# Holding first statistics behind an earlier supertile's places, and starting expert blocks one round earlier, in a fused AdaLN, scan and mixture-of-experts kernel

## Chip, cores and metric

The kernel runs on one core of a Trainium2 chip. The metric is the device time in microseconds. Before the change three executions took 446.07, 444.80 and 445.12 us; the median is 445.12 us. A time is called different here when it differs by more than 0.3%, 1.3 us.

## What is computed

32 sequences of 256 tokens with 128 channels, float32. Two layers, each behind a normalization that is modulated by a small conditioning vector:

```
mod = silu(c) @ wmod                        # six vectors for each sequence
h   = layernorm(x) * (1 + ca) + sa
g, a, v = sigmoid(h Wg' + bg), sigmoid(h Wd' + bd), h Wv' + bv
x   = x + ga * (scan(h_t = a_t h_{t-1} + (1 - a_t) v_t) * g)
h   = layernorm(x) * (1 + cb) + sb
logits = h @ gate_w' + gate_b               # 8 experts, the best 2 of a token
x   = x + gb * sum over 2 experts of prob_e * (relu(h w1[e] + b1[e]) w2[e] + b2[e])
```

Each token goes to its two best experts only, so the kernel has to sort tokens by expert, multiply, and bring the results back.

## The kernel before, in words

The 8192 tokens are cut into 16 **supertiles** of 512. A supertile passes four steps, which the code calls n, m, r and R:

- **n**, `a_norm` (L343): the statistics of the first normalization on VectorE (`stats` L303: four `bn_stats`, L307, and four `bn_aggr`, L311), a reciprocal root in some eleven small VectorE operations (`rsqrt`, L315 to L336), and four ScalarE activations that make `xn` (L355). Supertiles 12 and 13, and 14 and 15, share one root (`LN1G`, L62).
- **m**, `a_mix` (L364): transposes, three matmuls `pz` (L377), gates, and the scan on VectorE (L396).
- **r**, `a_res` (L400): the residual, the second statistics `stb`/`mvb` and root, and `xm` on ScalarE (L413).
- **R**, `a_route` (L416): logits on TensorE (`pl`, L428), best two experts, prefix counts (`pq`, L454), and then the **place** of each pair of token and expert in a region in DRAM. The cast to `pi` (L471) ends the placing. Eight indirect DMAs on GpSimd then scatter 128 rows each to `reg` (`send` L482, issued at L499).

`HEAD` (L33) writes down the first rounds: `n0|m0 n1|r0 m1 n2|R0 r1 m2 n3|...`. Round t handles n of supertile t, m of t-1, r of t-2 and R of t-3. In the first seven rounds R comes first in its round; from round 7 on n comes first and R last. r, m and R carry a priority ahead of program order (`AHEAD`, L39), n does not. The instructions of each engine are put into a fixed order when the program is built, by priorities and an estimate of times; on the chip each engine runs its list in order.

Routed rows are used in **blocks** of 256 rows of one expert. `b_load` (L579) has SyncE fetch the block's rows (`xr`, L584) and its expert's weights (`ww`, L590); `b_in` (L593) transposes and splits the rows (`xs`), `b_up` (L608) is twelve matmuls and the relu, `b_down` (L628) sixteen matmuls and the scaling `yt` (L639), and two scatters of results to `yd` on GpSimd. A load waits for the last sixteen row scatters that were sent before it in the program (L586). A row fetch is not told apart by expert: any of these rows could belong to it.

`b_step` (L729) runs one step of the block pipeline: loads up to four blocks ahead, `b_in` of block i, `b_up` of i-1, `b_down` of i-2. Between the supertile steps `between()` calls it, from round `FIRST` on, except at every eighth place, and only while more than two blocks are known and not begun. Blocks become known when supertiles 2 to 8, 10 and 12 are routed and their rows sent (`TAKE`, L30). `drip` (L507) sends row scatters, a few after each supertile step.

All scatters, of rows and of results, are chained in one written order (`scatter`, L497), and GpSimd runs them one after another. After the last route the remaining blocks run one after another; then SyncE loads the two results of each token (`c_load` L698) and VectorE adds them to x (`c_add` L709).

The lines that the change touches, in `stats`, `a_norm` and `a_route`:

```python
w = nc.vector.bn_stats(st[:, j], src[:, j])                       # L307
if behind:
    tc.add_manual_dep(w.ins, behind.name, ORDER, ...)             # L309
...
stats(mv[:, i * T:(i + 1) * T], xa[:, s + i], f"a{s + i}", placed[-1] if placed else None)   # L348
...
w = nc.vector.tensor_copy(pi, pf.rearrange("p t k -> p (t k)"))   # L471
if s < EARLY:
    placed.append(w.ins)
```

`ORDER` is an order on the same engine, without a semaphore: the statistics stand behind that cast in VectorE's list. `EARLY` is 3, so `placed` holds the casts of supertiles 0, 1 and 2.

Of the kernel before, what the change touches and what calls it, by code (L numbers as in the profile page):

```python
# [17 lines left out]
ORDER = mybir.DependencyInfo(mybir.DependencyClass.NoSync, mybir.DependencyReason.DATA)  # L18
# [8 lines left out]
T = 4  # L27
# [6 lines left out]

XE = 3
EARLY = 3
PW = 3

AHEAD = (0, 200, 300, 400)  # L39
# [1 line left out]
BACK = 2  # L41
SKIP = 8

FIRST = 6
THREE = 7

ALWAYS = 68
# [18 lines left out]
def adaln_moe(ctx: ExitStack, tc: tile.TileContext, x, Wg, bg, Wv, bv, Wd, bd,  # L66
# [16 lines left out]
    of = out.rearrange("b s d -> (b s) d")  # L83
# [23 lines left out]
    xa = cp.tile([P, NS, T, D], F32, name="xa")  # L107
# [189 lines left out]
    f = nc.sync.dma_start(reg[E * CAP:E * CAP + BLK].rearrange("(p t) d -> p t d", p=P), pad)  # L297
# [5 lines left out]
    def stats(mv, src, name, behind=None):  # L303
        n = src.shape[1]
        st = wk.tile([P, T, 6], F32, tag=f"st{name[0]}", name=f"st{name}")
        for j in range(n):
            w = nc.vector.bn_stats(st[:, j], src[:, j])  # L307
            if behind:
                tc.add_manual_dep(w.ins, behind.name, ORDER, reason="not ahead of the first supertiles that route")  # L309
        for j in range(n):  # L310
            nc.vector.bn_aggr(mv[:, j], st[:, j])  # L311

    def rsqrt(mv, name, s):

        n = mv.shape[1]  # L315

        def t1(nm, dt=F32):
            return wk.tile([P, n, 1], dt, tag=f"{nm}{name[0]}{n}", name=f"{nm}{name}")

        v, y, r = t1("nv"), t1("ny"), t1("nr")  # L320
        if s < PW:
            nc.vector.tensor_scalar(v, mv[:, :, 1:2], 1e-5, RSQ ** -2, op0=ALU.add, op1=ALU.mult)
            nc.gpsimd.tensor_tensor(y, v, mh[:, :n], op=ALU.pow)
        else:
            t = t1("nt")
            nc.vector.tensor_scalar(v, mv[:, :, 1:2], 1e-5, None, op0=ALU.add)
            nc.vector.tensor_scalar(y.bitcast(I32), v.bitcast(I32), 1, None, op0=ALU.logical_shift_right)
            nc.vector.tensor_scalar(y.bitcast(I32), y.bitcast(I32), -1.0, float(0x5f3759df), op0=ALU.mult, op1=ALU.add)
            nc.vector.tensor_tensor(t, y, y, op=ALU.mult)
            nc.vector.tensor_tensor(t, t, v, op=ALU.mult)  # L330
            nc.vector.scalar_tensor_tensor(t, t, -10.0 / 3.0, t, op0=ALU.add, op1=ALU.mult)
            nc.vector.scalar_tensor_tensor(y, t, 5.0, y, op0=ALU.add, op1=ALU.mult)
            nc.vector.tensor_tensor(t, y, y, op=ALU.mult)
            nc.vector.scalar_tensor_tensor(t, t, -0.5 * RSQ ** -2, v, op0=ALU.mult, op1=ALU.mult)
            nc.vector.scalar_tensor_tensor(y, t, 1.5, y, op0=ALU.add, op1=ALU.mult)
        nc.vector.scalar_tensor_tensor(r, mv[:, :, 0:1], -1.0, y, op0=ALU.mult, op1=ALU.mult)  # L336
        return y, r


    placed = []  # L340
    ln1 = {}

    def a_norm(s):  # L343
        g = LN1G.get(s, 0)
        if g:
            mv = wk.tile([P, g * T, 2], F32, tag=f"mva{g}", name=f"mva{s}")
            for i in range(g):
                stats(mv[:, i * T:(i + 1) * T], xa[:, s + i], f"a{s + i}", placed[-1] if placed else None)  # L348
            y, r = rsqrt(mv, f"a{s}", s)
            for i in range(g):  # L350
                ln1[s + i] = (y[:, i * T:(i + 1) * T], r[:, i * T:(i + 1) * T])
        y, r = ln1[s]
        xn = wk.tile([P, T, D], F32, tag="xn", name=f"xn{s}")
        for j in range(T):
            nc.scalar.activation(xn[:, j], xa[:, s, j], AF.Identity, scale=y[:, j], bias=r[:, j])  # L355
        return dict(s=s, xn=xn)

    def early(s, tag, name, bufs=1):

        if s < EARLY:  # L360
            return psb.tile([P, ST], F32, tag=tag, name=name, bufs=bufs)
# [38 lines left out]
    def a_res(a):  # L400
        s, og = a["s"], a["og"]
        xt = xa[:, s]
        po = early(s, "pbx", f"po{s}")
        for j in range(T):
            nc.tensor.transpose(po[:, j * P:(j + 1) * P], every(og, j), ident)
        xm = xt.rearrange("p t d -> p (t d)")
        nc.vector.tensor_tensor(xm, po, xm, op=ALU.add)
        mv = wk.tile([P, T, 2], F32, tag="mvb", name=f"mvb{s}")
        stats(mv, xt, f"b{s}")
        y, r = rsqrt(mv, f"b{s}", s)  # L410
        xn = wk.tile([P, T, D], F32, tag="xm", name=f"xm{s}")
        for j in range(T):
            nc.scalar.activation(xn[:, j], xt[:, j], AF.Identity, scale=y[:, j], bias=r[:, j])  # L413
        a["xn"] = xn

    def a_route(a, base):  # L416
        s, xn = a["s"], a["xn"]
# [51 lines left out]
        nc.vector.tensor_reduce(pf, op_, axis=AX.X, op=ALU.add)  # L469
        pi = wk.tile([P, T * K], I32, tag="pi", name=f"pi{s}", bufs=3)  # L470
        w = nc.vector.tensor_copy(pi, pf.rearrange("p t k -> p (t k)"))  # L471
        if s < EARLY:
            placed.append(w.ins)
        sm = wk.tile([P, T], F32, tag="sm", name=f"sm{s}")
        nc.vector.tensor_reduce(sm, e8, axis=AX.X, op=ALU.add)
        rc = wk.tile([P, T], F32, tag="rc", name=f"rc{s}")
# [30 lines left out]
    def drip(n):  # L507
        for _ in range(min(n, len(sending))):
            s, send, j, k = sending.pop(0)
            w = send(j, k)  # L510
            sent.append(w)
            if not sending or sending[0][0] != s:
                while held and held[0][0] <= s:
                    blocks.extend(held.pop(0)[1])
# [252 lines left out]
    def between():  # L767
        nonlocal slot
        slot += 1
        if slot % SKIP and len(blocks) - len(flow) > BACK:  # L770
            b_step()
# [19 lines left out]
    for t, todo in enumerate(steps):  # L791
        def step3(s):
            nonlocal base, done
            with tc.high_priority(AHEAD[3] * (s >= EARLY)):
                base = a_route(st[s], base)
                if s in CLS:
                    b = cp.tile([P, E], F32, name=f"cnt{s}")
                    nc.vector.tensor_copy(b, base)  # L798
                    base = b
                    counts.append(b)  # L800
                nb = len(blocks) + sum(len(x) for _, x in held)
                if s in TAKE:
                    n = full(s) - nb
                    tb, done = table(s, counts[:1] * (s > CUT) + [base], done, n, False)
                    held.append((s, [(tb, q, []) for q in range(n)]))
                elif s == NS - 1:
                    n = touched(s) - nb
                    tb, done = table(NS, counts, done, n, True)
                    fills(base)
                    rest = [(tb, q, []) for q in range(n)]  # L810
                    held.append((s, rest))
                    z = 0
                    for c in CLS:
                        u = max(E, touched(c) - nb) if c == CUT else touched(c) - nb
                        rest[u - 1][2].extend(range(z, c + 1))
                        z = c + 1

        def step2(s):
            with tc.high_priority(AHEAD[2] * (s >= EARLY)):
                a_res(st[s])  # L820

        def step1(s):
            with tc.high_priority(AHEAD[1] * (s >= EARLY)):
                a_mix(st[s])

        def step0(s):
            with tc.high_priority(AHEAD[0] * (s >= EARLY)):
                st[s] = a_norm(s)

        for i, s in todo:  # L830
            (step0, step1, step2, step3)[i](s)
            drip(3 if t < THREE else 2 if len(sending) > K * T else 1)
            if t >= FIRST:
                between()
# [59 lines left out]
```

## Time and profile before

| | us |
|---|---|
| median of the runs | 445.12 |
| the profiled execution | 444.96 |
| its span, first to last instruction | 443.2 |
| TensorE busy / weight loads | 366.6 / 321.5 |
| VectorE busy | 326.2 |
| ScalarE busy | 291.5 |
| GpSimd busy | 285.0 |
| one scatter of rows, mean, x128 | 0.986 |
| one scatter of results, mean, x136 | 1.013 |
| mean granted TensorE clock | 0.904 of full speed |

How to read it: the span is one execution as the profiler of the chip saw it; what the measured time has more, 1.76 us, lies before the first and behind the last instruction. A busy share is an average over stages. In this kernel they differ: a head in which supertiles are normalized and routed and no block is ready (to about 95 us), a long middle in which routes and blocks share the engines (to about 320), blocks alone (to about 375), and blocks beside the sums. PE in the profile is TensorE's matmuls, PEld its weight loads, DVE is VectorE, ACT ScalarE, POOL GpSimd, SP SyncE. The page's slices cut the span in 40 pieces of 11.08 us and give the busy tenths of each.

Places (the cast of L471) and first row scatters of the first supertiles, from the timeline:

| supertile | place, start us | first row scatter, start us |
|---|---|---|
| 2 | 65.33 | 66.27 |
| 3 | 88.08 | 89.00 |
| 4 | 116.93 | 117.35 |
| 5 | 130.18 | 131.14 |
| 6 | 145.14 | 149.47 |

### The profile page before, as it was taken

What the parts mean: (1) busy time and instruction counts of PE and PEld (TensorE: products, weight loads), DVE (VectorE), ACT (ScalarE), POOL (GpSimd) and SP (SyncE); (2) the same over time, 40 slices, a digit from 0 to 9 for tenths busy, and PEclk for the clock granted to TensorE, in tenths of its full rate; (3) what the DMA queues carried; (4) which work ended last, traced back from release to release, by engine and by line L of the source; (5) the groups of instructions that cost most, each with busy time, mean ns of one, the idle gap of its engine ahead of it and who ended that gap; (6) DMA issues with size and microseconds to landing.
All of it is one profiled execution on the core that took longest, in us unless ns stands there. A gap on an engine that the chain in (4) does not pass through costs nothing.

```text
span 443.2 us, 11140 instructions
## 1 busy us (share of the span) xinstructions
PE 366.6 (83%) x2713; PEld 321.5 (73%) x2713; DVE 326.2 (74%) x1752; ACT 291.5 (66%) x721; POOL 285.0 (64%) x300
## 2 busy tenths in 40 slices
PE   4766465469999999999999999999389997499950
PEld 3333241328899889889989999999279997499940
DVE  6778889998878989978878877977337630346675
ACT  3765363476988998989778777666236666177630
POOL 4644857070577777777777777777777777555560
PEclk9988566588999999999999999999879999699995
DMA  7998311048438475655553886686189774799996
GB/s 196 370 321 248 137 42 45 4 123 297 150 96 246 124 209 169 182 161 173 172 173 114 260 277 197 185 275 173 50 265 304 219 221 148 233 342 362 352 271 197
DMA packets 54357, 89.59 MB, mean 202 GB/s; under 512 B 8366, under 2 KB 39292, under 8 KB 54294
## 3 DMA queue, kind: packets, MB, share of 16 engines
q1 hardware_dynamic: 44656, 70.87, 53.4%
q0 software_dynamic: 8480, 16.93, 10.8%
q10 hardware_dynamic: 1158, 1.07, 0.7%
q8 instruction: 25, 0.41, 0.4%
q14 instruction: 38, 0.31, 0.2%
HBM read 62.32 MB, written 27.04 MB: 202 GB/s over the span
## 4 chain that ended last, share of the span: by engine, by line
PE 57%; DMA 14%; DVE 11%; issue 6%; ACT 4%; POOL 4%; SPq 3%; POOLq 0%; DVEq 0%; ACTq 0%
PE pby L635 21%; PE pz L377 6%; PE p L617 6%; PE p L618 6%; PE p L619 6%; DMA yk<-yd 4%; DMA yd<-yt,xi 4%; PE pbx L597 3%; PE pl L428 3%; POOL reg L499 2%; DMA reg<-rw,pi 2%; PE pb L431 2%; DMA wr<-in_L_ffn_w_dram 2%; ACT xm L413 1%; POOL yd L499 1%
## 5 line engine op out<-in xcount | busy, mean ns | idle before, releaser
L499 POOL DMA_INDIRECT yd<-yt,xi x136 | 137.8, 1013 | 66.5 <-ACT yt L639 30.0
L499 POOL DMA_INDIRECT reg<-rw,pi x128 | 126.2, 986 | 61.6 <-issue 41.9
L635 PE MATMUL pby<-wr,hh 128*128 x1088 | 150.5, 276 | 0.3 <-ACT hh L625 0.3
L635 PEld LDWEIGHTS pby<-wr,hh 128*128 128x128 f32 x1088 | 137.7, 192 | 9.3 <-issue 6.9
L625 ACT ACTIVATE hh<-p,ww 128x256 f32<-128x256 f32 x219 | 93.1, 474 | 28.6 <-PE p L619 21.8
L617 PE MATMUL p<-xs,ww 128*128 128x256 f32 x272 | 86.2, 317 | 1.2 <-DVE cnt L798 0.3
L618 PE MATMUL p<-xs,ww 128*128 128x256 f32 x272 | 78.2, 288 | 0.0
L619 PE MATMUL p<-xs,ww 128*128 128x256 f32 x272 | 77.9, 287 | 0.0
L377 PE MATMUL pz<-h,wT 128*128 128x512 f32 x96 | 58.6, 728 | 3.7 <-ACT h L372 2.2
L639 ACT ACTIVATE yt<-pby,xr 128x128 f32<-128x128 f32 x136 | 42.7, 367 | 24.3 <-PE pby L635 24.3
L617 PEld LDWEIGHTS p<-xs,ww 128*128 128x128 f32 x272 | 52.5, 193 | 3.5 <-ACT ta L381 1.1
L618 PEld LDWEIGHTS p<-xs,ww 128*128 128x128 f32 x272 | 53.0, 195 | 0.5 <-issue 0.5
L619 PEld LDWEIGHTS p<-xs,ww 128*128 128x128 f32 x272 | 52.6, 193 | 0.2 <-issue 0.2
L597 PE MATMUL pbx<-ident,xr 128*128 128x128 f32 x136 | 27.1, 282 | 21.2 <-DMA xr<-reg 11.9
L600 DVE TENSOR_TENSOR xs<-pbx,xs 128x256 fp32r<-128x256 f32 x68 | 28.3, 416 | 20.4 <-ACT xs L599 20.2
L599 ACT ACTIVATE xs<-pbx 128x256 fp32r<-128x256 f32 x68 | 26.4, 388 | 20.2 <-PE pbx L597 20.1
L413 ACT ACTIVATE xm<-xa,nrb,nyb 128x128 f32<-128x128 f32 x64 | 26.5, 484 | 12.8 <-DVE nrb L336 12.8
L714 DVE TENSOR_TENSOR ot<-yk 128x512 f32<-128x512 f32 (+1 forms) x17 | 11.2, 658 | 31.4 <-DMA yk<-yd 30.8
L597 PEld LDWEIGHTS pbx<-ident,xr 128*128 128x128 f32 x136 | 17.1, 146 | 23.5 <-issue 9.9
L377 PEld LDWEIGHTS pz<-h,wT 128*128 128x128 f32 x96 | 19.4, 232 | 19.7 <-issue 12.9
L355 ACT ACTIVATE xn<-xa,nra,nya 128x128 f32<-128x128 f32 x64 | 26.4, 488 | 6.5 <-DVE nra L336 6.5
L623 DVE TENSOR_SCALAR hh<-p,ww 128x256 f32<-128x256 f32 x53 | 25.2, 476 | 5.0 <-ACT hh L625 4.7
(195 smaller groups left out, 645.8 us busy)
## 6 DMA issues: line engine op xcount, KB each, us to landing
ww<-wd SPq DMA_DIRECT2D x68, 514.0 KB
xr<-reg SPq DMA_DIRECT2D x68, 130.0 KB
yk<-yd SPq DMA_DIRECT2D x30, 256.0 KB
wd<-wh SPq DMA_DIRECT2D x8, 514.0 KB
xa<-in_L_attn_x_dram SPq DMA_DIRECT2D x16, 256.0 KB
out_dram<-ot SPq DMA_DIRECT2D x12, 256.0 KB
yd<-yt,xi POOLq DMA_INDIRECT x136
w1s<-in_L_ffn_w_dram SPq DMA_DIRECT2D x8, 256.0 KB
```

Of the source, the lines that this page charges most:

```text
L355: nc.scalar.activation(xn[:, j], xa[:, s, j], AF.Identity, scale=y[:, j], bias=r[:, j])
L377: nc.tensor.matmul(z, wT[:, i], h1, start=True, stop=True)
L413: nc.scalar.activation(xn[:, j], xt[:, j], AF.Identity, scale=y[:, j], bias=r[:, j])
L499: w = nc.gpsimd.indirect_dma_start(in_offset=None, **args).ins
L597: nc.tensor.transpose(px[:, j * P:(j + 1) * P], xr[:, j, 0:D], ident)
L600: w = nc.vector.tensor_tensor(xs[:, 1], px, xs[:, 0], op=ALU.subtract)
L617: nc.tensor.matmul(z, hi, xs[:, 0], start=True, stop=False)
L618: nc.tensor.matmul(z, hi, xs[:, 1], start=False, stop=False)
L619: nc.tensor.matmul(z, lo, xs[:, 0], start=False, stop=True)
L625: nc.scalar.activation(hh[:, k], p1[:, k - k0], AF.Relu, bias=bias)
L635: nc.tensor.matmul(py[:, j * D:(j + 1) * D], hh[:, k, j * P:(j + 1) * P], we[:, k * D:(k + 1) * D], start=(j == 0 and k == 0), stop=(j == ...
L639: nc.scalar.activation(yt[:, j], py[:, j * D:(j + 1) * D], AF.Copy, scale=xr[:, j, D:D + 1])
```

## The change

Two things. `placed` now takes the cast of every supertile, and the first statistics of supertile s stand behind the cast of supertile s-5, or of supertile 2 where s-5 is less than that, or of the last one written so far where that is earlier still. And blocks may go between the steps from round 5 on, not 6.

```diff
+BEHIND = 5
...
-FIRST = 6
+FIRST = 5
...
-                stats(mv[:, i * T:(i + 1) * T], xa[:, s + i], f"a{s + i}", placed[-1] if placed else None)
+                stats(mv[:, i * T:(i + 1) * T], xa[:, s + i], f"a{s + i}", placed[min(len(placed) - 1, max(s - BEHIND, EARLY - 1))] if placed else None)
...
         w = nc.vector.tensor_copy(pi, pf.rearrange("p t k -> p (t k)"))
-        if s < EARLY:
-            placed.append(w.ins)
+        placed.append(w.ins)
```

For supertiles 0 to 7 the cast is the one that it was. Supertile 8 now stands behind the cast of 3, 9 behind 4, 10 behind 5, 11 behind 6, 12 and 13 (one group) behind 7, 14 and 15 behind 9. A comment string of the order was reworded; nothing else changes.

More of the change, by code (lines that the diff above doesn't have):

```diff
@@ L308, in stats @@
             if behind:
-                tc.add_manual_dep(w.ins, behind.name, ORDER, reason="not ahead of the first supertiles that route")
+                tc.add_manual_dep(w.ins, behind.name, ORDER, reason="not ahead of earlier supertiles that route")
         for j in range(n):
```

## The prediction

> **What bounds the kernel now.** I read the shares, then the 40 slices, then the order of GpSimd's work, then its waits by stretch.
>
> ```profile
> span 443.2 us, 11140 instructions
> PE 366.6 (83%) x2713; PEld 321.5 (73%) x2713; DVE 326.2 (74%) x1752; ACT 291.5 (66%) x721; POOL 285.0 (64%) x300
> PE   4766465469999999999999999999389997499950
> POOL 4644857070577777777777777777777777555560
> ```
>
> The shares name PE. The slices name two engines: from about 110 us PE shows 9 and POOL an unbroken 7. What the 7 is shows in the timeline of GpSimd (start, duration, operation, idle before and what ended it):
>
> ```profile
> 375.94 0.98 POOL L499 DMA_INDIRECT yd<-yt,xi  x1 [0.30 <-DMA yd<-yt,xi]
> 377.22 0.98 POOL L499 DMA_INDIRECT yd<-yt,xi  x1 [0.30 <-DMA yd<-yt,xi]
> ```
>
> A scatter takes 0.98 us and the next starts 0.30 us later, whatever is named: 1.28 us a scatter, and 0.98/1.28 = 0.77 is the digit 7. From 117.35 to 383 us no idle before a scatter is longer, but for one of 0.98 at 131. GpSimd is **saturated for 266 us**. Its 264 scatters (128 of routed rows, 136 of results) follow one written order, which I walked from the loops. Up to block 52's results, that stretch is 1.3 us times the scatters in it. Block 52's results matter because the SyncE queue waits there, at the first load of summed results (378.2 us), with two more block loads behind it.
>
> The rule that speaks against this is in the Trainium skill, "Perfetto Trace Analysis", § Identifying the Most-Contended Engine: the engine with the highest occupancy is to be optimized, TensorE judged by its weight loads. Those are busy 58.8 of 60 us in 250-310, GpSimd 45.8, so the rule names PE, and an earlier start of the scatters would earn nothing by itself. The trace answers with what happens when supertile 15's last rows go out at 318.64:
>
> ```profile
> 313.45 0.39 PE L635 MATMUL pby<-wr,hh 128*128 x2
> 323.31 0.66 PE L597 MATMUL pbx<-ident,xr 128*128 128x128 f32 x2 [9.47 <-DMA xr<-reg]
> ```
>
> PE is idle for 9.5 us for rows that were placed at 275.5 and lay 43 us in GpSimd's line. By the rule the change would give only what PE gains in the head; by the row the scatters decide, and PE may gain up to 9.5 us less than they do without harm. I take the row.
>
> So what can be won is **GpSimd's idle time before 117 us**:
>
> ```profile
> 76.00 0.95 POOL L499 DMA_INDIRECT reg<-rw,pi  x1 [0.30 <-issue]
> 89.00 0.95 POOL L499 DMA_INDIRECT reg<-rw,pi  x1 [12.05 <-issue]
> ...
> 111.77 0.99 POOL L499 DMA_INDIRECT yd<-yt,xi  x1 [12.69 <-ACT yt L639]
> 113.07 0.99 POOL L499 DMA_INDIRECT yd<-yt,xi  x1 [0.30 <-issue]
> 117.35 0.96 POOL L499 DMA_INDIRECT reg<-rw,pi  x1 [3.29 <-DVE stb L307]
> ```
>
> The first gap ends with the place of supertile 3 (the cast to pi at 88.08), the second with block 0's result, the third with supertile 4's place (116.93). Less 0.30 each, that is 11.75 + 12.39 + 2.99, and 0.68 at 131: 27.8 us, the most that the change can bring.
>
> **Part 1, statistics held back.** Before, every first statistic from supertile 5 on has to follow only supertile 2's place (65.33). The timeline of VectorE has the statistics of 5 to 15, eleven supertiles, between 65.41 and 94.1, and VectorE is busy 46.96 of the 51.8 us from 65.3 to 117.1. [...] One supertile costs 14.83/11 = 1.35 us for the four statistics and four aggregates (the time on tile sta in that window over eleven), and some 0.8 for the eleven small operations of its root, which start 0.07 apart when interleaved: about 2.15 us.
>
> Supertile 3's path: its second statistics start at 63.82, its root ends only at 75.44, interleaved with 5 to 8; then ScalarE and PE lead to the logits at 82.61 (four activations each for 3, 5 and 6 stand between); then VectorE to the place at 88.08, with aggregates, roots and statistics of 11 and 12 between. What is barred on it is 8's four statistics in the first stretch (0.9) and about 2.0 in the last (seven aggregates and statistics and four small operations). The rest lies beside ScalarE. Gain 3 us: place 3 at 85, its rows from 86.0 to 96.1.
>
> Supertile 4's path, 88.08 to 116.93: on tile sta VectorE spends 4.36 + 0.37 us from 88.2 to 107.1, and the roots some 3.5 more, all of 9 to 15, all barred now; 8's 2.15 comes in. Net 6 us; with the 3 from supertile 3, place 4's first row goes from 117.35 to 108.4.
>
> What is moved is paid later: 9 to 15 put seven times 2.15 us, 15 us less two roots, beside the full rounds, 2.15 to a round. A round of places is 15 us there (130.18, 145.14, 161.09), VectorE busy 60.83 of 69. It fits, but the lag of GpSimd behind the places is only 0.9 us at supertile 5 (131.14 for 130.18) and 4.3 at 6, so the first round is late by 2.15 - 0.9 = 1.2 us. After that the lag covers it.
>
> Does VectorE's work slow the scatters beside it? "SBUF — State Buffer" of the Trainium skill (the "DVE blocks DMA" trap) says that two-port fast modes, which copies and tensor-scalar operations can enter, lock GpSimd out of writing descriptors. The deferred roots hold three such operations of 0.15 us, five roots in all: 2.3 us at most. The row: scatters of results start 1.28 apart at 370-378, with VectorE idle, and rows 1.26 apart at 240-246 beside it. I take nothing, and 2.3 for the range.
>
> **Part 2, blocks one round earlier.** Block steps now start after the mix of supertile 4 in the fifth round, not after the route of 3 in the sixth. A load waits for the last sixteen scatters sent before it in the program. Before, three of these are supertile 3's (load at 94.31, 2.79 us after the third at 91.52). After, the walk gives supertile 2's last, at 76.00: load at 78.8. SyncE's queue is empty from 52 to 94, so nothing is queued behind this wait that anyone needs. From load to result block 0 takes 111.77 - 94.31 = 17.46 us; it then comes at 96.3, just as supertile 3's rows end. The second gap closes. Block 1's result is ready 6.4 us later (ScalarE, 111.13 and 117.52), at 102.7, and goes out before supertile 4; today it goes at 126.6.
>
> Engines have room for three blocks there: PE is busy 5.9 of 10 us in 80-90, ScalarE 4.1; VectorE pays about 1.0 us a block (0.42 + 0.47 + 0.15), which part 1 has freed. TensorE's granted clock is 0.50 in 80-90; more work may raise it, and I count nothing for that. The walk also shifts the skipped places and puts one step fewer before the last route, so supertile 15's last row is scatter 188, not 190. That moves 2.6 us from one side of it to the other; block 52 stays at its count.
>
> **Sum.** Supertile 4's first row 9.0 us earlier; block 1's two scatters now in front of it, not behind, 2 x 1.3 = 2.6; less 1.2. Gain 10.4 us. The saturated stretch carries it to the SyncE wait at 378, and the rest follows. 443.2 - 10.4 = 432.8 span; the profiled execution has 1.76 around it (444.96), so 434.6, and its time is 0.16 under the median of 445.12: **434.7 us**.
>
> **Rivals.**
> - *The whole gap goes* (0.12). The static order on VectorE is remade, supertiles 3 and 4 come 12 us apart like 4 and 5 (13 us), place 3 several us earlier. Against: supertile 3's middle is ScalarE and PE. 18 to 24 of the 27.8 us: about 424.
> - *VectorE becomes the bound* (0.16). Deferred statistics stretch the early rounds, and half of the head's gain is given back. For: VectorE 0.88 busy there. Against: the growing lag. A gain of 3 to 5: about 441.
> - *Blocks stand in front of the routes* (0.18), slower. Queues are in order. If block 0's matmuls are put ahead of supertile 3's logits, these wait for weights, which landed about 4.5 us after their issue (94.94, first use 99.43): 79.5 + 4.5, plus 3 us of matmuls, so 87 instead of 80.7. That is 6.5 us late, which eats part 1's gain. If the same happens to supertile 4 with blocks 2 and 3 (another 7 us of PE), its rows go from 108.4 to 123: about 449. It decides from a total delay of 11 us on.
> - *Nothing moves* (0.04), since the order barely changes: 445.
>
> The forecast, a gain of 6 to 16 us, has 0.50. A measurement of this kernel tells 0.3%, 1.3 us, from no change. Faster takes the forecast, the whole gap and VectorE's case, 0.50 + 0.12 + 0.16; same 0.04; slower 0.18. Range 425 to 447: the upper end takes in no change and part of the slower case, the lower most of the whole gap. The likeliest alone: 429 to 439.
>
> **What would show it.** Places 3 and 4 near 85 and 108; the first block load near 79; the gap before block 0's result under 3 us; scatters 1.28 apart from about 108; supertile 15's last row near 305; PE's hole before it still there or smaller. Wrong if place 4 is not earlier, if PE waits for weights inside routes 3 or 4, or if GpSimd shows new gaps between 110 and 200.

## The result, and the profile after

The changed kernel takes **466.46 us** (median of four runs, 465.65 to 468.19) beside 445.27 for the kernel before on the same chip: a ratio of 1.0467, 95% interval 1.043 to 1.0505. The forecast was 434.7 us. On some of the chips used for the experiments every kernel here, the kernel before among them (587 to 598 us), took a third longer or more, so those runs are listed apart and the explanation rests on the others.

The page of the changed kernel, its span, shares and the slices of TensorE and GpSimd (busy tenths, 40 slices of 11.6 us):

```profile
span 464.3 us, 11105 instructions
PE 382.5 (82%) x2713; PEld 331.4 (71%) x2713; DVE 330.3 (71%) x1752; ACT 294.2 (63%) x721; POOL 287.1 (62%) x300
PE   4757773999969959999997999967999995399950
POOL 3644855270427777777777375777777777746560
```

PE's row of nines now starts two slices earlier, at about 81 us, and has holes where it had none (6, 5, 7, 6, 7). POOL's unbroken 7 now starts later, with a 0 in front of it at 104 to 116 us, and is broken by a 3 and a 5. GpSimd's line was to be saturated earlier. It is saturated later. Its timeline (start, duration, idle time before and what ended it; where it is more than 1 us, GpSimd has paused):

```profile
89.92 0.95 POOL L500 DMA_INDIRECT reg<-rw,pi  x1 [12.39 <-ACT xs L600]
...
100.02 1.00 POOL L500 DMA_INDIRECT yd<-yt,xi  x1 [0.31 <-ACT h L374]
...
103.90 0.98 POOL L500 DMA_INDIRECT yd<-yt,xi  x1 [0.30 <-ACT hh L626]
121.26 0.96 POOL L500 DMA_INDIRECT reg<-rw,pi  x1 [16.39 <-ACT hh L626]
...
139.85 0.96 POOL L500 DMA_INDIRECT reg<-rw,pi  x1 [8.52 <-issue]
...
266.06 0.96 POOL L500 DMA_INDIRECT reg<-rw,pi  x1 [7.19 <-ACT h L374]
...
284.58 0.96 POOL L500 DMA_INDIRECT reg<-rw,pi  x1 [3.05 <-ACT hh L626]
```

The results of blocks 0 and 1 do go out directly behind supertile 3's rows, at 100 to 105 us: the pause in front of block 0's result is gone. But supertile 4's first row comes at 121.26 instead of 117.35, after a pause of 16.39 us. Supertile 5's first row has to wait another 8.52, and later the line runs dry in front of supertiles 12 and 13. Supertile 15's last row goes out at 336.28 (before: 318.64), block 52's result at 394.37 (374.65), 19.7 us late; the span is 21.1 us longer.

Where TensorE's time went instead shows in the busy time by stretch. First the kernel before, then the changed one (stretch, its length, then busy us and, in brackets, instructions of each engine; behind them the granted clock):

```profile
89.00:105.00 16.00, 12.02 (x44) 6.54 (x45) 14.67 (x104) 12.07 (x28) 7.94 (x8) 0.90 0.63 200
105.00:121.00 16.00, 16.00 (x115) 14.55 (x116) 13.21 (x111) 12.85 (x33) 4.86 (x5) 0.89 0.61 190
121.00:140.00 19.00, 19.00 (x156) 17.55 (x155) 16.71 (x106) 16.47 (x40) 14.22 (x14) 1.00 0.52 147
```

```profile
89.00:105.00 16.00, 15.92 (x112) 13.12 (x111) 11.69 (x75) 14.37 (x38) 11.60 (x12) 1.00 0.43 132
105.00:121.00 16.00, 16.00 (x142) 15.51 (x141) 13.42 (x71) 13.23 (x34) 0.00 (x0) 1.00 0.43 135
121.00:140.00 19.00, 14.58 (x93) 11.84 (x92) 15.44 (x114) 11.63 (x28) 8.08 (x9) 0.80 0.37 108
```

Before, PE had 4 us to spare in 89 to 105 and nothing from 105 to 140. After, it is full from 89 to 121 while GpSimd has no instruction at all from 105 to 121, and it is idle for 4.4 us in 121 to 140. So TensorE did work that the scatters had no use for yet, and then lacked work when GpSimd at last handed rows out.

Which work, its timeline tells (`pbx` is the start of a block, `ph`, `pl` and `pq` are a supertile's transposes, logits and prefix counts; a selection from 80 to 89 and 108 to 119 us):

```profile
81.03 0.69 PE L598 MATMUL pbx<-ident,xr 128*128 128x128 f32 x2 [3.02 <-DVE nra L338]
81.51 1.71 PE L430 MATMUL pl<-cols,hT 128*128 128x8 f32 x8
84.40 0.66 PE L598 MATMUL pbx<-ident,xr 128*128 128x128 f32 x2
87.00 0.26 PE L456 MATMUL pq<-mk,tri 128*128 128x40 bf16 x1
...
110.24 0.60 PE L422 MATMUL ph<-ident,xm 128*128 128x128 f32 x4
112.71 0.38 PE L598 MATMUL pbx<-ident,xr 128*128 128x128 f32 x2
...
117.19 0.38 PE L598 MATMUL pbx<-ident,xr 128*128 128x128 f32 x2
118.55 0.18 PE L456 MATMUL pq<-mk,tri 128*128 128x40 bf16 x1
```

The first `pbx` stands ahead of supertile 3's logits, and the one at 117.19 is the ninth. The order in which TensorE starts its work is that of the list written at build. Cut to what matters it reads (b stands for the transposes that start a block; with the supertile's number, h are the transposes, L the logits and Q the counts of the route, o the transposes of step r, x and z those and the matmuls of step m):

```
before   h3 L3 Q3 o4 x5 z5 x6 b0 z6 o5 b1 h4 L4 b2 x7 b3 Q4 o6 z7 b4 h5 b5 L5 x8 b6 Q5
changed  h3 b0 L3 b1 Q3 o4 b2 x5 b3 z5 x6 b4 z6 b5 o5 b6 h4 b7 L4 b8 Q4 x7 o6 z7 h5 L5 b9 Q5
```

Four blocks stood in front of supertile 4's counts, now nine do. Blocks have the lower priority, but the list is written with an estimate of when each input is there, and a block can be put in wherever a supertile's next step is taken to wait for another engine.

### The profile page after: what moved, and what is told of

It reads as the page before. It is cut to its first block, busy times and chain, and to the rows that moved or that the text cites. A ratio compares the mean times of both kernels' runs of the same rounds, so it can differ in the third digit from the quotient of the medians.

```text
span 464.3 us, 11105 instructions
## 1 busy us (share of the span) xinstructions
PE 382.5 (82%) x2713; PEld 331.4 (71%) x2713; DVE 330.3 (71%) x1752; ACT 294.2 (63%) x721; POOL 287.1 (62%) x300
## 4 chain that ended last, share of the span: by engine, by line
PE 59%; DVE 13%; DMA 12%; ACT 7%; issue 4%; SPq 3%; POOL 1%; POOLq 0%; ACTq 0%; DVEq 0%
PE pby L636 22%; PE p L618 7%; PE p L619 6%; PE p L620 6%; PE pz L379 4%; PE pbx L598 4%; PE pl L430 3%; DMA yd<-yt,xi 2%; ACT xm L415 2%; PE pb L433 2%; DMA ww<-wd 2%; ACT xn L357 2%; DMA wr<-in_L_ffn_w_dram 1%; PE po L407 1%; DMA xr<-reg 1%
## 5 line engine op out<-in xcount | busy, mean ns | idle before, releaser
L500 POOL DMA_INDIRECT yd<-yt,xi x136 | 139.8, 1028 | 53.5 <-issue 21.9
L636 PE MATMUL pby<-wr,hh 128*128 x1088 | 154.2, 279 | 0.4 <-ACT hh L626 0.2
L636 PEld LDWEIGHTS pby<-wr,hh 128*128 128x128 f32 x1088 | 140.0, 195 | 7.6 <-issue 5.3
L626 ACT ACTIVATE hh<-p,ww 128x256 f32<-128x256 f32 x219 | 94.3, 475 | 38.4 <-PE p L620 29.5
L618 PE MATMUL p<-xs,ww 128*128 128x256 f32 x272 | 89.0, 331 | 3.0 <-DMA ww<-wd 1.7
L619 PE MATMUL p<-xs,ww 128*128 128x256 f32 x272 | 79.5, 293 | 0.0
L620 PE MATMUL p<-xs,ww 128*128 128x256 f32 x272 | 78.8, 290 | 0.0
L618 PEld LDWEIGHTS p<-xs,ww 128*128 128x128 f32 x272 | 53.8, 200 | 5.9 <-issue 2.9
L619 PEld LDWEIGHTS p<-xs,ww 128*128 128x128 f32 x272 | 54.1, 199 | 1.2 <-issue 1.2
L620 PEld LDWEIGHTS p<-xs,ww 128*128 128x128 f32 x272 | 53.4, 196 | 0.5 <-issue 0.5
L598 PE MATMUL pbx<-ident,xr 128*128 128x128 f32 x136 | 28.8, 296 | 25.7 <-DVE xs L601 12.9
```

What stands on the lines that cost most here:

```text
L500: w = nc.gpsimd.indirect_dma_start(in_offset=None, **args).ins
L598: nc.tensor.transpose(px[:, j * P:(j + 1) * P], xr[:, j, 0:D], ident)
L618: nc.tensor.matmul(z, hi, xs[:, 0], start=True, stop=False)
L619: nc.tensor.matmul(z, hi, xs[:, 1], start=False, stop=False)
L620: nc.tensor.matmul(z, lo, xs[:, 0], start=False, stop=True)
L626: nc.scalar.activation(hh[:, k], p1[:, k - k0], AF.Relu, bias=bias)
```

## The experiments

Three theories run through them. **A**: the work of the early blocks stands in front of the routes and delays them. **B**: the statistics that are held back come in the way later. **C**: a block whose rows are not yet written heads TensorE's list, and a route waits behind it.

**The two parts apart.** Part 1 alone is the change without the new `FIRST`, part 2 alone is the kernel before with it:

```diff
# part 1 alone                     # part 2 alone
-FIRST = 5                         -FIRST = 6
+FIRST = 6                         +FIRST = 5
```

> Only the first part: statistics behind the place five supertiles in front, blocks from round 6 as before. Where the kernel before takes 445, Theory A (early blocks in front of the routes did the harm): place 4 comes 5 to 10 us earlier than 116.9 and the time is 434 to 445. Theory B (deferred statistics did it): rounds of places grow by 2 us each, 455 to 466. Theory C (each part remakes TensorE's list so that a block whose rows come late heads the line in front of a route): single waits of TensorE for rows of 2 to 10 us, 447 to 466. Where the kernel before takes 590 to 594, as in the four runs above, 4% more again.

Part 1 alone: 444.03 us (442.22 to 445.45) beside 445.15, ratio 0.9965 [0.9941, 0.999].

> Only the second part: blocks from round 5, statistics as before. With the first part alone at 444.0 where the kernel before takes 445, the early blocks have to bring the loss: blocks 0 to 7 stand in front of supertile 4's prefix counts in TensorE's list, place 4 at 113 to 122, single waits of TensorE of 2 to 4 us for rows behind it, gaps of GpSimd of 5 us and more after 105; 455 to 470. If only the two parts together lose (early blocks cost nothing without deferred statistics): 440 to 447.

Part 2 alone: 457.52 us (457.18 to 460.64) beside 444.72, ratio 1.0313 [1.0257, 1.0368].

The time is as A said; place 4 comes at 124.98 us, later than its 113 to 122. So no loss comes without part 2, and B falls as a cause by itself: held back alone, the statistics cost nothing. But together the parts cost 21 us, more than the 12.8 of part 2 alone. In front of supertiles 3 to 5 GpSimd pauses as long in both (37.1 and 37.3 us); it is in front of 12 and 13 that the change pauses 10.2 us and part 2 alone 4.2, and what is due to the held-back statistics there is open.

GpSimd's pauses in part 1 alone:

```profile
85.91 0.95 POOL L500 DMA_INDIRECT reg<-rw,pi  x1 [9.49 <-issue]
106.95 0.99 POOL L500 DMA_INDIRECT yd<-yt,xi  x1 [10.98 <-ACT yt L640]
110.01 0.96 POOL L500 DMA_INDIRECT reg<-rw,pi  x1 [0.78 <-DVE nb L533]
127.27 0.95 POOL L500 DMA_INDIRECT reg<-rw,pi  x1 [4.78 <-ACT h L374]
```

Supertiles 3 and 4 come 3.1 and 7.3 us earlier, as intended, and in front of supertile 5 there is a pause of 4.78 (0.98 before) that takes about half of the second gain back. And its pauses in part 2 alone, in front of supertiles 3 and 4:

```profile
96.90 0.97 POOL L499 DMA_INDIRECT reg<-rw,pi  x1 [21.81 <-ACT yt L639]
...
125.91 0.96 POOL L499 DMA_INDIRECT reg<-rw,pi  x1 [13.74 <-ACT xs L599]
```

Here blocks hold up supertile 3 itself: 21.81 instead of 12.05 us. In TensorE's list of this kernel block 0 stands in front of its logits, and blocks 1 to 3 in front of its counts.

**Block 9 behind supertile 5's counts.** Both parts, with one more known block kept in hand in the first rounds. Nine blocks stay in front of supertile 4's counts; block 9 moves from in front of supertile 5's counts (`L5 b9 Q5`) behind them (`L5 Q5 ... b9`):

```diff
-        if slot % SKIP and len(blocks) - len(flow) > BACK:
+        if slot % SKIP and len(blocks) - len(flow) > (BACK if t > 7 else 3):
```

> The kernel with both parts that keeps three known blocks in hand before supertile 8, once more. Theory A, the work of nine blocks in front of route 4 is the loss: place 4 stays at 119 to 122 us with GpSimd's idle time before it at 14 to 18, and the time is 458 to 466 us. Theory C, the block with late rows at the head of TensorE's line is the loss: the 8.5 us of idle time before supertile 5's first row falls below 4, and the time is 445 to 455 us.

461.82 us (461.36 to 462.01) beside 445.04, ratio 1.0385 [1.0352, 1.0417]. In the changed kernel the block's transposes waited for rows, with the counts behind them:

```profile
134.98 0.69 PE L598 MATMUL pbx<-ident,xr 128*128 128x128 f32 x2 [3.86 <-DMA xr<-reg]
135.46 0.24 PE L456 MATMUL pq<-mk,tri 128*128 128x40 bf16 x1
```

Here GpSimd's pauses in front of supertiles 4, 5 and 12 are:

```profile
120.21 0.96 POOL L500 DMA_INDIRECT reg<-rw,pi  x1 [19.08 <-ACT hh L626]
135.66 0.96 POOL L500 DMA_INDIRECT reg<-rw,pi  x1 [2.78 <-issue]
...
262.92 0.96 POOL L500 DMA_INDIRECT reg<-rw,pi  x1 [8.23 <-ACT h L374]
```

The 8.52 in front of supertile 5 fell to 2.78, as C said, but the time fell by some 4 us only (4.6 by the medians; 3.6 by the ratios, as the chips differ). C is real at this place and is the smaller part; place 4 stayed at 119.25, as A said.

**Both parts, without the crowd.** Five known blocks kept in hand in the first rounds (`else 5` in the line above). TensorE's list then has three blocks in front of supertile 4's counts and none in front of supertile 3's:

> The kernel with both parts that keeps five known blocks in hand before supertile 8, once more. Theory A, the work of nine blocks in front of route 4 is what is left of the loss: place 4 at 107 to 111 us, idle time of GpSimd before supertile 4's first row below 3 us, time 440 to 450 us. Theory B, the later statistics: above 455. Theory C, blocks with late rows head the line wherever they stand: the stall before supertile 12's first row stays at about 8 us and the time is 450 to 458 us.

446.97 us (445.6 to 449.68) beside 444.4, ratio 1.0058 [1.0027, 1.0089]. The time is in A's range; the stall is not where A had it. Place 4 comes at 113.19, and since block 0's result (120.52) is now behind supertile 4's first rows in the line, two pauses of before have become one:

```profile
114.13 0.96 POOL L500 DMA_INDIRECT reg<-rw,pi  x1 [18.23 <-issue]
```

18.23 us, where the kernel before has 12.69 + 3.29 = 15.98. The pauses in front of supertiles 12 and 13 are gone.

Place 4 is 3.6 us later than in part 1 alone (109.57), although one block fewer stands in front of it. TensorE's timeline shows C at work here too:

```profile
99.42 0.69 PE L598 MATMUL pbx<-ident,xr 128*128 128x128 f32 x2 [4.30 <-DMA xr<-reg]
```

Block 0 is drawn later in this kernel and its load goes out at 97.24 (90.97 in part 1 alone). TensorE stands idle in front of it for 4.30 us, with supertile 4's transposes behind it in the list: they come at 105.20 instead of 100.14. So the number of blocks alone does not set place 4: one block whose rows are late, in front of a step of the route, delays it as well.

**The early start with fewer blocks.** Blocks still from round 5, but only three drawn before round 9. The list then has five blocks in front of supertile 4's counts, block 0 still in front of supertile 3's logits:

```diff
-        if slot % SKIP and len(blocks) - len(flow) > BACK:
+        if slot % SKIP and len(blocks) - len(flow) > BACK and (t > 8 or len(flow) < 3):
```

> The changed kernel, with its blocks still from round 5 on, but at most three drawn before round 9. TensorE's list then has five blocks (0 to 4) in front of supertile 4's counts instead of nine, block 0 still in front of supertile 3's, none between those of supertiles 4 and 5, and block 26 last in front of supertile 12's (30 in the changed kernel, 27 in the kernel before). Theory A, the number of blocks in front of the routes is the loss: place 4 comes near 105 to 110 us instead of 120, GpSimd's idle time before supertile 4's first row falls from 16 us to below 9 and that before supertile 5's below 4, and the kernel takes 436 to 448 us. If the early start itself is the loss (block 0 in front of supertile 3's counts, rows late for what stands in front), it stays above 455.

452.42 us (450.95 to 453.61) beside 446.76, ratio 1.0137 [1.0078, 1.0197]: 14 us better than the changed kernel, 4 us worse than hoped at most. Place 4 comes at 116.63, not 105 to 110, and GpSimd's pauses in front of supertiles 4 and 5 are:

```profile
117.56 0.96 POOL L500 DMA_INDIRECT reg<-rw,pi  x1 [17.93 <-ACT h L374]
129.37 0.96 POOL L500 DMA_INDIRECT reg<-rw,pi  x1 [1.90 <-issue]
```

So drawing fewer blocks takes back most of the loss, and the early start itself costs something too: the timeline has supertile 4's transposes at 110.58, as late as with nine blocks (110.24). Blocks 0 to 4 lie in front of them in both, and 5 and 6 only in the changed kernel; but the matmuls of blocks in front of them (up and down, without transposes), counted in the traces, are 140 here and 136 there. Here all five blocks are worked to their end in front of these transposes; in the changed kernel seven are begun and the last ones are left in part for later. The five kernels with 136 to 140 such matmuls there have these transposes at 109.2 to 110.7, the kernel before and part 1 alone, with 12, at 102.5 and 100.1. So it is the work in front of the step that goes with its delay, not the number of blocks begun. Between the transposes and the counts no block is left here, which brings the counts to 115.44 instead of 118.55. And this kernel has written out only 27 blocks' results by supertile 15's last row, where the kernel before has 31, so more is left for the end.

**Later blocks one route back.** The changed kernel has block 30 in front of supertile 12's counts, the kernel before block 27. This edit takes the list back to block 27 there and leaves it as it is up to supertile 9's counts:

```diff
-        if slot % SKIP and len(blocks) - len(flow) > BACK:
+        if slot % SKIP and len(blocks) - len(flow) > BACK and (not 11 < t < 15 or len(flow) < 4 * t - 32):
```

> The changed kernel with the later blocks held one route back (rounds 12 to 14), a third time. Theory A, the nine blocks in front of route 4 are the whole loss: 464 to 468 us. Theory C, blocks one route too early are a loss of their own at supertile 12: the idle times of 7.2 us before supertile 12's first row and 3.1 before supertile 13's go, those of 16 and 8.5 us before supertiles 4 and 5 stay, and the time is 454 to 459 us.

471.32 us (468.8 to 472.18) beside 444.69, ratio 1.057 [1.0501, 1.064]: slower than the changed kernel, which neither theory said. The pause in front of supertile 12 is gone, as C had it, but pauses in front of 10 and 13 are there instead:

```profile
230.87 0.95 POOL L500 DMA_INDIRECT reg<-rw,pi  x1 [4.57 <-issue]
285.01 0.96 POOL L500 DMA_INDIRECT reg<-rw,pi  x1 [7.55 <-ACT hT L426]
```

The edit changed more than it was meant to: a block step that isn't drawn also sends no row and no result, so GpSimd's written order shifted too (block 13's result at 212.49, behind supertile 9's first row; 203.07 and in front of it in the changed kernel). What the pauses in front of supertiles 12 and 13 are due to is therefore **not settled**. Against a cause of their own speaks that they are gone in the two kernels that put fewer blocks in front of supertile 4; but these put fewer in front of supertile 12 as well (28 and 27, where the change has 31).

The traces show where the time goes, though. From supertile 5's place to supertile 12's, first in the kernel before, then in the changed one (columns as above):

```profile
130.18:238.12 107.94, 107.76 (x859) 97.39 (x859) 92.82 (x546) 93.94 (x239) 81.98 (x83) 1.00 0.60 175
136.57:265.13 128.56, 119.08 (x865) 105.54 (x865) 102.14 (x643) 97.69 (x240) 91.29 (x92) 0.92 0.57 170
```

Seven rounds, with 21 blocks begun in both, take 20.6 us longer. TensorE is idle for 9.5 us where it had 0.2, 5.5 of it for the rows of blocks, and is busy 11.3 us longer with about the same number of instructions: its granted clock is 0.92 instead of 1.00. It is low in three stretches, 0.53 in 132 to 143, 0.57 in 166 to 174 and 0.57 in 255 to 263, and at the beginning of each or just before it TensorE has waited (3.86 us for rows; 2.73 for rows and 2.44 for ScalarE; 2.75 for rows). So a wait for rows seems to cost more than its own length. In the same rounds the granted clock is 1.00 in part 1 alone and with five blocks kept, 0.97 with three drawn before round 9, and 0.92 to 0.94 in the four kernels that pause in front of supertile 12 or 13. That is C, with the clock behind it, but read from the traces alone: no run took these waits away and left the rest.

**One account for all.** Every kernel sends the same 264 scatters. The table has, for each, the sum of GpSimd's pauses of more than 0.6 us in front of its scatters 25 to 190 (from supertile 3's first row on; in the kernel before to supertile 15's last):

| kernel | blocks in front of supertile 4's counts | pauses, us | against before | span against before |
|---|---|---|---|---|
| before | 4 | 29.0 | | |
| part 1 alone | 4 | 26.0 | -3.0 | 0.0 |
| both, five kept | 3 | 29.6 | +0.6 | +1.7 |
| both, three drawn before round 9 | 5 | 34.0 | +5.0 | +7.7 |
| part 2 alone | 8 | 41.3 | +12.3 | +12.3 |
| both, three kept | 9 | 45.2 | +16.2 | +16.8 |
| the change | 9 | 47.5 | +18.5 | +21.1 |
| the change, later blocks back | 9 | 55.7 | +26.7 | +27.3 |

The span follows the pauses within 3 us in every row. Up to scatter 190 that is bookkeeping, since scatters and pauses make up GpSimd's time; what the table adds is that the time behind scatter 190 is about the same in all eight, 123 to 126 us. Of the change's 18.5 us, 8.3 lie in front of supertiles 3 to 5 and 10.2 in front of 12 and 13. In part 1 alone the 3.0 us that the pauses lose are used up by the scatters themselves: those 166 are busy for 167.1 us instead of 164.3. By its medians part 1 alone is still the fastest kernel of all that ran, 0.35% [0.1, 0.59] under the kernel before, which is at the edge of what can be told from no change.

**The runs on chips where everything took longer.** The kernels are the ones above; the ratios are to the kernel before on the same chip.

| kernel | us | before | ratio |
|---|---|---|---|
| part 2 alone | 618.45; 614.19; 617.19 | 594.22; 590.7; 595.5 | 1.043 [1.0371, 1.049]; 1.0355 [1.0271, 1.0439]; 1.0345 [1.0254, 1.0436] |
| part 1 alone | 619.62; 616.36 | 594.22; 590.7 | 1.045 [1.0387, 1.0514]; 1.042 [1.0343, 1.0497] |
| both, three kept | 620.4; 621.79 | 594.22; 593.81 | 1.045 [1.0397, 1.0503]; 1.0464 [1.0382, 1.0547] |
| both, five kept | 600.08; 599.84; 595.72 | 594.22; 595.5; 586.53 | 1.0093 [1.006, 1.0127]; 1.0085 [1.0042, 1.0128]; 1.0167 [1.0117, 1.0216] |
| the change, later blocks back | 611.36; 620.1 | 588.22; 597.55 | 1.0412 [1.0373, 1.0451]; 1.0491 [1.0384, 1.0597] |

What was expected of them, by kernel. Part 2 alone:

> Only the second part of the change: blocks from round 5, statistics as before. Theory A, blocks in front of the routes: TensorE's list has blocks 0 to 7 in front of supertile 4's prefix counts (before: 0 to 3), so place 4 stays at 115 to 122 although blocks start near 79, the routes run late, and the time is 455 to 470. Theory B, the deferred statistics did the harm: this kernel has none of them deferred, so it is at most 446, with place 4 near 112.

> Only the second part of the change: blocks from round 5, statistics as before. Theory A, blocks in front of the routes: TensorE's list has blocks 0 to 7 in front of supertile 4's prefix counts (before: 0 to 3), so place 4 stays at 115 to 122 although blocks start near 79, and the time is 455 to 470 where the kernel before takes 445. Theory B, the deferred statistics did the harm: this kernel has none deferred, at most 446.

> Only the second part: blocks from round 5, statistics as before. With the first part alone at 444.0, the early blocks have to bring the loss. Where the kernel before takes 445: blocks 0 to 7 stand in front of supertile 4's prefix counts in TensorE's list, place 4 at 113 to 122, TensorE with single waits of 2 to 4 us for rows behind it and GpSimd with gaps of 5 us and more after 105; 455 to 470. If instead only the two parts together lose (the early blocks cost nothing without deferred statistics), 440 to 447.

Part 1 alone:

> Only the first part: statistics behind the place five supertiles in front, blocks from round 6 as before. Blocks 0 to 3 stand in front of supertile 4's prefix counts, as before. Theory A: place 4 comes 5 to 10 us earlier than the 116.9 of before, and the time is 434 to 445. Theory B: the rounds from supertile 5 on grow by 2 us each, GpSimd gets gaps between 130 and 250, and the time is 455 to 466.

> Only the first part: statistics behind the place five supertiles in front, blocks from round 6 as before; blocks 0 to 3 in front of supertile 4's prefix counts, as before. Theory A: place 4 comes 5 to 10 us earlier than 116.9 and the time is 434 to 445. Theory B: rounds of places from supertile 5 on grow by 2 us, GpSimd gets gaps between 130 and 250, 455 to 466. Theory C, each part costs by itself because a remade list puts a block whose rows come late in front of a route: TensorE shows single waits of 2 to 10 us for rows in both kernels, and both lie between 447 and 466.

Both, three kept:

> Both parts, but before round 8 a block goes between only while more than three are left, not two, so that block steps end one earlier in the seventh round: TensorE's list still has blocks 0 to 8 in front of supertile 4's prefix counts, but block 9, whose rows come late, is no longer in front of supertile 5's. If the nine blocks' own work in front of supertile 4 is the harm, about as slow as the changed kernel, 458 to 467. If the one block at the head of the line is, place 5 comes 4 us earlier and the time is 450 to 458.

> Both parts of the change, but before supertile 8 a block may be drawn only while more than three known ones are left, not two. TensorE's list then still has nine blocks (0 to 8) in front of supertile 4's counts, but block 9, whose rows come from supertile 4's last row, no longer stands in front of supertile 5's counts: it follows them. Theory A, the work of nine blocks in front of route 4 is the loss: place 4 stays at 119 to 122 us and GpSimd's idle time before it at 14 to 18, and the kernel takes 458 to 466 us, ratio 1.03 to 1.05. Theory C, a block with late rows at the head of the line is the loss: the 8.5 us idle time before supertile 5's first row falls below 4, no TensorE wait of over 1 us for block 9's rows is left near 135, and the kernel takes 445 to 455 us, ratio 1.00 to 1.022. Theory B, the later statistics are the loss: no change from the changed kernel's 466.

Both, five kept:

> Both parts, but before round 8 a block goes between only while more than five are left: blocks start as late as before (first load after supertile 3's rows), and TensorE's list has 0 to 2 in front of supertile 4's prefix counts. Statistics deferred as in the change. Theory A: the harm is gone, 434 to 446. Theory B: still 455 or more.

> Both parts, but before round 8 a block goes between only while more than five are left, so that blocks start as late as before and 0 to 2 stand in front of supertile 4's prefix counts. If early blocks are the harm: 438 to 447, places 3 and 4 near 85 and 109 as with the first part alone. If the deferred statistics and the other skips still do harm: 450 or more.

> Both parts of the change, but before supertile 8 a block may be drawn only while more than five known ones are left. TensorE's list then has three blocks (0 to 2) in front of supertile 4's counts, where the changed kernel has nine and the kernel before four; none of them stands in front of supertile 3's counts. Theory A, the work of nine blocks in front of route 4 is what is left of the loss: place 4 comes at 107 to 111 us, GpSimd's idle time before supertile 4's first row falls from 16 us to below 3, and the kernel takes 440 to 450 us, ratio 0.988 to 1.011. Theory B, the later statistics cost it: above 455. Theory C, blocks whose rows come late head the line wherever they stand: the stall of about 8 us in front of supertile 12's first row is still there and the kernel takes 450 to 458 us.

The change, later blocks back:

> The changed kernel with one edit: in rounds 12 to 14 a block may be drawn only while fewer than 4t - 32 have been, which leaves TensorE's list as it is up to supertile 9's counts (nine blocks in front of supertile 4's, block 9 in front of supertile 5's) and puts block 27 last in front of supertile 12's counts, as in the kernel before, where the changed kernel has block 30. Theory A, the nine blocks in front of route 4 are the whole loss: 464 to 468 us as the changed kernel. Theory C, at supertile 12 a second loss is made by blocks whose rows GpSimd has yet to write: the idle times of 7.2 us before supertile 12's first row and 3.1 before supertile 13's go, those of 16 and 8.5 before supertiles 4 and 5 stay, and the time is 454 to 459 us.

> The changed kernel with the later blocks held one route back (rounds 12 to 14), once more. Theory A, the nine blocks in front of route 4 are the whole loss: 464 to 468 us. Theory C, blocks one route too early are a loss of their own at supertile 12: the idle times of 7.2 us before supertile 12's first row and 3.1 before supertile 13's go, those of 16 and 8.5 us before supertiles 4 and 5 stay, and the time is 454 to 459 us.

Most of these expectations took the kernel before at 445 us, and their times were missed for that reason. On these chips part 1 alone loses as much as part 2 alone, 4%, and elsewhere nothing, so the split found above is not shown to hold there. GpSimd's line isn't full there either: in part 1 alone it pauses 172 us in front of scatters 25 to 190 (26.0 on the other chips), each of which takes 0.96 us there too. The cause is open, and no step of the explanation rests on these runs.

## Why the prediction was wrong

**That the scatters decide: right.** The prediction set GpSimd's row against the rule of the Trainium skill's "Perfetto Trace Analysis", § Identifying the Most-Contended Engine, which named PE. By the account above the span follows GpSimd's pauses in all eight kernels. But in another sense the rule was right to point at PE: PE is the engine without room (16.00 of 16 us in 105 to 121), and the pauses in front of supertiles 4 and 5 end when routes come that stood behind blocks in PE's list. The scatters are the bound, and PE's order decides what feeds them.

**Part 1 at supertiles 3 and 4: right.** Place 3 was to be at 85 and is at 84.98 in part 1 alone; supertile 4's first row was to be at 108.4 and is at 110.01.

**Part 1's cost later: the term was mis-sized.** The prediction took 1.2 us for the first full round. In part 1 alone supertile 5's place comes 16.8 us behind supertile 4's (109.57, 126.33), where the kernel before needs 13.3, so 3.5 us of the lead are lost there, and GpSimd pauses 4.78. With the longer scatters (2.9 us) part 1 is worth 1.1 us by its medians and not the 9.0 - 1.2 = 7.8 of the sum. The 2.9 us are about the 2.3 that the prediction kept for the trap of "SBUF — State Buffer"; but of the 13 scatters over 1.2 us in 80 to 336 us six lie beside a small root operation and five beside a scan, so they are not shown to be that trap.

**Part 2's loads and results: right.** The first block load was to go out at 78.8 and went at 78.88. Block 0's result was to be ready at 96.3, in time for the end of supertile 3's rows; it is ready at 94.3 and goes out at 100.02 directly behind them. Block 1's was to be ready at 102.7 in front of supertile 4; it is ready at 101.2 and goes out at 102.61.

**"Engines have room for three blocks there": the step that failed.** It read PE's room in 80 to 90 us, 5.9 of 10 busy, and costed three blocks there at nothing. Two things were wrong in it. It was not three blocks: every block that is known when the list is written may go where the list has room, and nine went in front of supertile 4's counts. And the place was not 80 to 90: a block's sixteen matmuls down and twelve up follow two and one steps behind its transposes, so the work fell into 88 to 121. There the trace of the kernel before, which the prediction had, shows 12.02 of 16 and 16.00 of 16 us busy. A block takes PE about 4 us (blocks 6 and 7 start at 108.85 and 112.71), so five more in front of supertile 4's counts are some 20 us of work, an estimate, for the 7.8 us that PE had idle from 80 to 121 (33.20 of 41 busy).

Its effect on supertile 4 can be followed on PE, in part 1 alone:

```profile
100.14 0.60 PE L422 MATMUL ph<-ident,xm 128*128 128x128 f32 x4
108.16 0.19 PE L456 MATMUL pq<-mk,tri 128*128 128x40 bf16 x1
```

With part 2 added, supertile 3's counts go from 83.86 to 87.00 (3.1 us), supertile 4's transposes from 100.14 to 110.24 (7.0 more, blocks 2 to 6 between) and its counts from 108.16 to 118.55 (0.3 more). Together 10.4 us, and the place goes from 109.57 to 120.31. That is all of part 1's gain at supertile 4 and 3.4 us beyond. Then the line starves: with the earlier blocks used up, block 9 is the next one known, its rows are supertile 4's own, which are late, and supertile 5's counts stand behind it.

**The rival that came true was sized too low.** "Blocks stand in front of the routes" had 0.18 and 449 us, for blocks 0 to 3. It named the wait for weights as its lever, and in 80 to 140 us of the changed kernel that wait is small (0.56 us, once, at 137.30; in part 2 alone 1.32 at 81.07 and 2.08 at 113.34); the work itself is the lever, and there were nine blocks of it. The scatters 1.28 us apart from 108 us on, supertile 15's last row near 305 and the span of 432.8 fell with it: block 0's pause of 12.69 us went, as forecast, but those in front of supertiles 4 and 5 grew from 3.29 and 0.98 to 16.39 and 8.52 us. The 10.2 us in front of 12 and 13, more than half of what the change adds in all, were in no case of the prediction. They go when fewer early blocks are drawn, but how these bring them about is open.

## What to carry to other kernels

An engine with a saturated line is only the bound while it is fed. Before work is started earlier, ask whether the engine that feeds the line has idle time in the very stretch into which the new work falls, and not only at its start. Where a list is written at build, letting work in one round earlier lets in all of that work that is known by then: count it in the new list, and see which step of the critical chain stands behind it. Here the routes hand GpSimd sixteen times eight row scatters, about 10 us of its line each, while a block of some 4 us on PE hands it two; so a block put in front of a route starves the line even if its own result comes early, and one whose own rows are late holds up the route with its wait as well (4.30 us with five blocks kept).

## What had not been expected of the hardware

Some scatters take much longer than 0.96 to 1.0 us: in 80 to 336 us 7 of 179 are over 1.2 us in the kernel before, 13 of 179 in part 1 alone, up to 1.73 us. Of these 20, 11 lay beside a scan on VectorE, while of all 358 only 53 did; 12 lay beside a small root operation, as did some 120 of all. That is a correlation, and no run took either away.

On the chips where all kernels took a third longer the granted TensorE clock of the profiled executions was 0.79 to 0.81 on the mean instead of 0.87 to 0.90. Part 1 alone has a span of 614.4 us there instead of 443.2, with VectorE busy as long (328.5 and 328.4 us) and TensorE longer (424.1 and 370.2 us); the rest is time in which the engines wait. Chips of the same number showed both at different times, so what sets it stays open.
